# Transposing the first pair by blocks on VectorE and through DRAM, in a fused attention and Fourier kernel

## The chip, the cores and the metric

The kernel runs on one core of a Trainium2 chip. The metric is the device time of one execution in microseconds. Before the change it is 3119.44 us, the median of three runs (3116.04 to 3120.33).

## The reference, cut to what matters

The input x has 4 images of 64 channels, 96 by 96 positions, in float32. Two layers follow each other, each added to its input.

```
# layer 0, on the group-normalised x (N = 9216 positions)
q, k, v  = wq x + bq, wk x + bk, wv x + bv     # 8, 8 and 64 channels
out      = v . sigmoid(q^T k)                  # an N x N matrix for each image
out      = out + x;  scale = sigmoid(mlp(mean(out)) + mlp(max(out)))
x        = x + out * scale

# layer 1, on the group-normalised result
u_hat    = rfft2(u)                            # 96 x 49 modes
v_hat    = per mode (c -> o) matrix, for 32 rows (16 low, 16 high) x 16 columns of modes; the rest is 0
x        = x + irfft2(v_hat)
```

Nearly all the work is the N x N matrix of layer 0. Layer 1 keeps 32 x 16 modes, so its transforms are two small matrix products: along w to 16 modes (real and imaginary, 32 columns) and along h to 32 modes.

## The kernel before, in words

Two images are a pair, and a pair fills the 128 partitions (2 images x 64 channels). `xs[p]` is a 128 x 9216 tile that holds pair p, with positions h, w along the free dimension. The attention of the first pair runs first, then that of the second.

**Tiles and blocks.** A pair's attention has 18 blocks of 512 query positions (36 in all). A block has 144 chunks: 72 groups of 128 keys for each of two images. Chunks are handled in tiles of 6 or 7: TensorE writes 6 or 7 PSUM banks of energies (line 441), ScalarE takes their sigmoid into `at` (line 452), TensorE multiplies `at` with the values into an accumulating bank (line 470). PSUM has 8 banks, one of which accumulates. So a tile of 7 fills PSUM, and a tile of 6 leaves one bank spare. A block follows one of three patterns: DENSE (24 tiles of 6), HALF (22 tiles, about half of them of 6) or SPARSE (21 tiles, three of them of 6). `pattern` (line 530) gives each block its own: the second pair's first 12 blocks are HALF, its last six SPARSE. There are 774 tiles. Block 18, the second pair's first, begins with tile 384, in the code `first`.

**Hidden work.** During the second pair's attention, layer 1 of the first pair is woven in (class `Hidden`, line 236). Its steps are put at tile numbers when the program is written: `put` (line 545) takes a list of steps and gives each the next free slot at or after a tile, where a slot is a tile whose successor has size 6, so that a bank is spare. These steps stand in `mid[t]`, between the energies of tile t+1 and the products of tile t. Work that needs no bank goes to `end[t]`. The main loop (lines 646 to 663) emits a tile at a time in this order, and `later` ties a step's VectorE instructions behind the last marked VectorE instruction of the attention. One slot in a block goes to the queries of the next block.

The steps in their order, with the tiles that `put` gives them:
- `result(s)`, 12 strips of 768 positions, at the ends of tiles 391, 393, ..., 413: load the strip of the original x into `old`, combine (line 162), write the sum to DRAM (`x1d`), and take statistics.
- `transposes(r)`, 24 steps from tile 393 on: TensorE transposes four rows h of the image, 128 x 96 each, into a bank, and VectorE copies them to `xT` (96 x 512).
- `along_w(m)`, 6 steps among the former: four matmuls with the 96 x 32 table `fw` into four groups of 32 partitions of one bank. VectorE copies the bank to `ae`, and the DMA takes it through DRAM (`ad`) into `ah`, where h lies on the partitions. The last is at tile 475.
- statistics at tiles 477 to 483, then `along_h(i)` at tiles 493, 495, 497, 499: 32 matmuls each with weights 96 x 64 out of `ah` and 64 columns of the table `fh`, and two scalings by VectorE into `ut`.
- `mix` (16 steps from tile 503), `back_h` (8 steps from 551) and `back_w` (24 steps from 581 to 639) multiply by the modes' matrices, whose weights are loaded four at a time, and transform back.

All of these DMAs are issued by the SyncE queue (SP), in order: an issue that waits holds those behind it. When a step's bank, its VectorE copy or its operand isn't ready, TensorE waits too, since it takes its instructions in order. [...]

Of the kernel before, what the change touches and what calls it, by code (L numbers as in the profile page):

```python
# [33 lines left out]
F32 = mybir.dt.float32  # L34
F32R = mybir.dt.float32r
AF = mybir.ActivationFunctionType
ALU = mybir.AluOpType
# [3 lines left out]
P = 128  # L41
B, C, H, W = 4, 64, 96, 96
# [4 lines left out]
KW = 16  # L47
KH = 32
NB = 512
NBLK = N // NB  # L50
# [4 lines left out]
DENSE = [6] * 24  # L55
HALF = [6 if i == 1 or i % 2 == 0 and i < 18 else 7 for i in range(22)]
SPARSE = [6 if i in (0, 1, 11) else 7 for i in range(21)]
LAG = 8
SIDE = 4
U = KH * KW * 4  # L60
UPAD = 4 * SIDE
STRIP = 8 * W
SQ = 32
NSQ = H // SQ
NSTRIP = N // STRIP
# [16 lines left out]
def tile_kernel(ctx: ExitStack, tc: tile.TileContext, x, cst, late, spec, out):  # L82
    nc = tc.nc
    xf = x.rearrange("b c h w -> (b c) (h w)")
# [5 lines left out]
    dram = ctx.enter_context(tc.tile_pool(name="dram", bufs=1, space=bass.MemoryType.DRAM))  # L90
# [3 lines left out]
    xs = []  # L94
    for p in range(NPAIR):
        xt = xpool.tile([P, N], F32, tag=f"x{p}", name=f"x{p}")
        for s in range(9):
            cols = bass.ts(s, N // 9)
# [7 lines left out]
    def named(name, rows=P):  # L106
        return cs[:rows, PLACE[name]]

    pav, nhalf, low_sb, ident = named("pav"), named("nhalf"), named("low"), named("ident")
# [126 lines left out]
    class Hidden(Layer1):  # L236


        def __init__(self, p, gate, bank, move, work):
            super().__init__(p, gate, bank, move, (nc.sync,) * 3)  # L240
            self.work = work
            self.stats = small.tile([P, 2 * NSTRIP, 6], F32, tag="stats1", name=f"stats1_{p}")
            self.xts, self.ah = {}, None
            self.ad = dram.tile([H, 2 * KW, P], F32, tag=f"ad{p}", name=f"ad_{p}")
            self.zd = dram.tile([H, 2 * KW, 2, C], F32, tag=f"zd{p}", name=f"zd_{p}")

# [4 lines left out]
            self.wts = (self.wts + rooms[:3]) * (KH // 8)  # L251
            self.place_of_vt = lambda: rooms[3]

        def result(self, s):
            p, cols = self.p, bass.ts(s, STRIP)
            old = self.work.tile([P, STRIP], F32, tag="old", bufs=2, name=f"old_{p}_{s}")
            nc.sync.dma_start(old, xf[bass.ts(p, P), cols])
            self.combine(s, old)
            for i in (2 * s, 2 * s + 1):
                nc.vector.bn_stats(self.stats[:, i, :], xs[p][:, bass.ts(i, STRIP // 2)])  # L260

        def stats_steps(self):
            mr, steps, _ = group_stats(self.stats, self.bank, f"l1_{self.p}")
            return steps + [lambda: self.spread(mr)]

        def transposes(self, r):

            pt = self.bank(f"pt_{self.p}_{r}")
            for i in range(4):
                nc.tensor.transpose(pt[:W, bass.ts(i, P)], xs[self.p][:, bass.ts(4 * r + i, W)],  # L270
                                    ident)
            self.xts[r] = self.work.tile([W, NB], F32, tag="xT", bufs=4, name=f"xT_{self.p}_{r}")
            self.move(self.xts[r], pt[:W, :])

        def along_w(self, m):


            pa = self.bank(f"pa_{self.p}_{m}")
            for g in range(4):
                nc.tensor.matmul(pa[bass.ts(g, 2 * KW), :], named("fw", W), self.xts[4 * m + g],  # L280
                                 start=True, stop=True)
            ae = self.work.tile([P, NB], F32, tag="ae", bufs=2, name=f"ae_{self.p}_{m}")
            self.move(ae, pa)
            if self.ah is None:
                self.ah = self.work.tile([P, 2 * KW * P], F32, tag="ah", name=f"ah_{self.p}")
            for g in range(4):
                nc.sync.dma_start(
                    self.ad[16 * m + 4 * g:16 * m + 4 * g + 4].rearrange("i k c -> k i c"),
                    ae[bass.ts(g, 2 * KW), :].rearrange("k (i c) -> k i c", c=P))
            rows = bass.ts(m, 16)  # L290
            nc.sync.dma_start(self.ah[rows, :],
                                     self.ad[rows].rearrange("h k c -> h (k c)"))

        def along_h(self, i):

            b, half = i // 2, i % 2
            ah = self.ah.rearrange("h (s k b c) -> h s k b c", k=KW, b=2, c=C)
            u = self.ut[:, :U].rearrange("q (h k n s b) -> q n k s h b", h=KH, n=SIDE, s=2, b=2)
            if i == 0:
                nc.vector.memset(self.ut[:, U:], 0.0)  # L300
            pu = self.bank(f"pu_{self.p}_{i}")
            fh = named("fh", H)
            for k in range(KW // 2):
                for s in range(2):
                    for part in range(2):
                        first = KH * (2 - s - part)
                        nc.tensor.matmul(pu[bass.ts(part, C), bass.ts(k, 2 * KH)],
                                         ah[:H, s, half * (KW // 2) + k, b, :],
                                         fh[:, first:first + 2 * KH],
                                         start=(s == 0), stop=(s == 1))  # L310
            v = pu.rearrange("q (n k s h) -> q n k s h", n=2, s=2, h=KH)
            for n in range(2):
                nc.vector.tensor_scalar(u[:, 2 * half + n, :, :, :, b], v[:, n],
                                        self.rs[:, 0, b:b + 1], None, ALU.mult)

        def weights(self, rows):
            for h in rows:
# [38 lines left out]
    with tc.tile_pool(name="work", bufs=1) as work, \  # L356
# [32 lines left out]
        def later(step):  # L389
            with tc.issue_after(mark[0].ins):  # L390
                step()
# [126 lines left out]
        each, norm0, _ = stats_of(0)  # L518
# [5 lines left out]
        q = queries(0, 0)  # L524
# [2 lines left out]
        keys(0, 1)  # L527
        values_of(0, 1)

        pattern = [DENSE] + [SPARSE] * (NBLK - 2) + [DENSE] + [HALF] * 12  # L530
        pattern += [SPARSE] * (NPAIR * NBLK - len(pattern))
        sizes = [size for sz in pattern for size in sz]
        starts = [sum(sz[:i]) for sz in pattern for i in range(len(sz))]
# [7 lines left out]
        end = [[] for _ in range(T)]  # L541
# [3 lines left out]
        def put(t, steps, every=1):  # L545

            for step in steps:
                t = next(f for f in free if f >= t)
                free.remove(t)
                mid[t] += [lambda step=step: later(step)]  # L550
                t += every
            return t

        ask = {}
        for n in range(1, NPAIR * NBLK):
            t = begins[n] - 4
            if pattern[n - 1] is DENSE:
                end[t] += [lambda n=n: ask.update({n: queries(n // NBLK, n % NBLK)})]
            else:
                t = [f for f in free if f < begins[n] - 1][-1]  # L560
# [15 lines left out]
        for s in range(NBLK):  # L576
            tiles = TILES * (NBLK - 1) + 8 * (s + 1)
            t = next(t for t in range(T) if done[t] >= tiles)
# [5 lines left out]
        first = begins[NBLK]  # L584
        gate, steps, _ = after(0)
        end[first + 1] += [lambda: later(steps[0])]
        put(first + 2, steps[1:], 2)
        l1 = Hidden(0, gate, bank_a, lambda dst, src: nc.vector.tensor_copy(dst, src), work)  # L588
        x1d = dram.tile([P, N], F32, tag="x1", name="x1d")
        for s in range(NSTRIP):  # L590
            end[first + 7 + 2 * s] += [lambda s=s: later(lambda: (
                l1.result(s), nc.sync.dma_start(x1d[:, bass.ts(s, STRIP)],
                                                xs[0][:, bass.ts(s, STRIP)])))]
        t = put(first + 9, [step for m in range(H // 16) for step in [
            lambda r=r: l1.transposes(r) for r in range(4 * m, 4 * m + 4)] + [
                lambda m=m: l1.along_w(m)]])
        t = put(t, l1.stats_steps(), 2)

        def workspace():
# [10 lines left out]
            l1.weights(range(5, 8))  # L610

        end[t] += [workspace]
        t = put(t + 2, [lambda i=i: l1.along_h(i) for i in range(4)], 2)
        end[t] += [more_room, lambda: later(l1.constant_mode)]

        def mixing(q, half):
            l1.mix(q, half)
            if half and q + 2 < KH // 4:
                l1.weights(range(4 * q + 8, 4 * q + 12))

        t = put(t + 1, [lambda q=q, half=half: mixing(q, half)
                        for q in range(KH // 4) for half in range(2)])
        t = put(t + 5, [lambda i=i: l1.back_h(i // 4, i // 2 % 2, i % 2) for i in range(8)])
        t = put(t + 5, [lambda i=i: l1.back_w(i, x1d) for i in range(H // 4)])


        early = []
# [1 line left out]
        def fetch():  # L629
            held = xpool.tile([P, N], F32, tag="x0", name="w_early")  # L630
            early.extend(held[:, bass.ts(i, KW * C)] for i in range(9))
            for i, w in enumerate(early):
                nc.gpsimd.dma_start(w, spec[NSLOT + i])
# [4 lines left out]
        for s in range(NSTRIP):  # L638
            tiles = TILES * (NPAIR * NBLK - 1) + 2 * (STRIP // P) * (s + 1)
            t = next(t for t in range(T) if done[t] >= tiles)  # L640
# [5 lines left out]
        for t in range(T):  # L646
            n = block[t]
            spare[0] = n % 2 * 7
            if t + 1 < T:
                if starts[t + 1] == 0:  # L650
                    q = ask[n + 1]
# [5 lines left out]
            old = sum(1 for pair, _ in items if t and 2 * pair < total[t - 1])  # L657
# [6 lines left out]
        gate, steps, f = after(1)  # L664
# [4 lines left out]
    with tc.tile_pool(name="tail", bufs=1, reuse_waits="tile") as tail, \  # L669
# [19 lines left out]
        fw = lc[:, :NSQ * P]  # L689
        fh = lc[:, NSQ * P:3 * NSQ * P].rearrange("q (s m) -> q s m", s=2)  # L690
# [5 lines left out]
        def occupy(n, behind, pool):  # L696
# [3 lines left out]
            with tc.issue_after(behind.ins):  # L700
                for _ in range(n):
# [3 lines left out]
        l1 = Layer1(1, gate, lambda name: small_bank.tile([P, NB], F32, tag="m", name=name),  # L705
                    evacuate, (nc.sync, nc.gpsimd, nc.scalar))
# [10 lines left out]
        pu = [pu_bank.tile([P, NB], F32, tag=f"u{b}", name=f"pu_{b}") for b in range(2)]  # L717
        along_h = []
        for s in range(NSTRIP):
            cols = bass.ts(s, STRIP)  # L720
# [6 lines left out]
            n, i = divmod(s, NSTRIP // NSQ)  # L727
            if i == 0:
                pa = pa_bank.tile([P, 2 * NB], F32, tag="a", name=f"pa_{n}", bufs=2)
            v = xt.rearrange("q (h n c) -> q n h c", n=NSQ, c=SQ)  # L730
# [187 lines left out]
```

## Time and profile before

| part | from the profile |
|---|---|
| span of the profiled execution | 3116.6 us, 43034 instructions |
| TensorE (PE) busy | 3072.2 us, 99% |
| ScalarE (ACT) busy | 2424.6 us, 78% |
| VectorE (DVE) busy | 397.0 us, 13% |
| DMA, mean over the span | 29 GB/s, 88.87 MB |
| granted TensorE clock | 0.995 |
| second pair's blocks without hidden steps | 79.4 us each |
| second pair's blocks with hidden steps | 83.2 to 90.7 us each |
| from the last block's end to the end of the span | about 90 us |

The page names a group of instructions by its line, engine, operation and tiles (out<-in). PE is TensorE's matmuls and PEld its weight loads, which overlap them. A matmul of float32 data appears as two records. "Idle before" is the time for which an engine stood still before the instructions of a group, with the engine or DMA that ended it. A duration of one matmul overlaps its neighbours', so the cost of a step is read best from the distance between the energies (line 441) of two tiles that follow each other.

### The profile page before, as it was taken

The numbers are of one execution on the slowest core, as the hardware profiler recorded it, in microseconds if no ns is written. First come the engines' busy times: TensorE is split into PE (matmuls) and PEld (weight loads), VectorE is DVE, ScalarE is ACT, GpSimd is POOL, SyncE is SP. The second block draws the span as 40 slices with busy tenths as digits, with TensorE's granted clock in tenths as the row PEclk, the third lists the DMA queues.
The fourth block names the chain that finished last, engine by engine and source line by source line (L and its number), as shares of the span: only waits on it lengthen the run. The fifth ranks groups of instructions, "written<-read, shape, count | busy, mean of one in ns | idle before, by whom it ended". The sixth has DMA issues, their size and how long they took to land.

```text
span 3116.6 us, 43034 instructions
## 1 busy us (share of the span) xinstructions
PE 3072.2 (99%) x19186; PEld 1147.4 (37%) x19186; DVE 397.0 (13%) x838; ACT 2424.6 (78%) x1585; POOL 24.5 (1%) x49
## 2 busy tenths in 40 slices
PE   6999999999999999999999999999999999999998
PEld 3433333333333333334433333333333333333335
DVE  5300000000000000002331110110101100000015
ACT  3788888888888888886777777777777788888871
POOL 0000000000000000000000000000000010000001
PEclk9999999999999999999999999999999999999998
DMA  3000000000000000000120010131210130000026
GB/s 143 1 1 1 1 1 1 1 1 1 1 1 1 1 1 1 1 1 1 41 88 14 8 36 13 52 125 44 36 34 31 41 120 1 1 1 1 6 74 216
DMA packets 39161, 88.87 MB, mean 29 GB/s; under 512 B 10336, under 2 KB 17248, under 8 KB 38880
## 3 DMA queue, kind: packets, MB, share of 16 engines
q1 hardware_dynamic: 31856, 61.88, 6.4%
q0 software_dynamic: 5344, 19.27, 1.7%
q10 hardware_dynamic: 1776, 4.97, 0.4%
q8 instruction: 150, 2.46, 0.3%
q14 instruction: 35, 0.29, 0.0%
HBM read 62.77 MB, written 23.33 MB: 28 GB/s over the span
## 4 chain that ended last, share of the span: by engine, by line
PE 97%; DVE 1%; DMA 1%; issue 0%; POOL 0%; SPq 0%; ACT 0%; POOLq 0%; DVEq 0%
PE banks L470 74%; PE banks L441 16%; PE banks L409 1%; PE banks L421 1%; PE banks L348 1%; PE banks L398 1%; PE banks L203 1%; DMA x<-in_x_dram 0%; PE py L825 0%; PE banks L270 0%; DVE x L162 0%; DMA old<-in_x_dram 0%; DMA vd<-vm 0%; DVE xt L724 0%; PE banks L326 0%
## 5 line engine op out<-in xcount | busy, mean ns | idle before, releaser
L452 ACT ACTIVATE at<-banks 128x1536 f32<-128x1536 f32 (+1 forms) x1548 | 2404.4, 1597 | 610.6 <-PE banks L441 546.8
L470 PE MATMUL banks<-at,vT 128*64 128x512 f32 (+1 forms) x11728 | 2395.2, 549 | 0.0
L470 PEld LDWEIGHTS banks<-at,vT 128*64 128x64 f32 x11728 | 780.4, 136 | 1348.9 <-issue 1294.1
L441 PE MATMUL banks<-q,kT 32*128 32x512 f32 x5184 | 571.4, 454 | 1.6 <-DVE xT L588 1.6
L441 PEld LDWEIGHTS banks<-q,kT 32*128 32x128 f32 x5184 | 232.9, 182 | 472.3 <-issue 301.5
L475 DVE SCALAR_TENSOR_TENSOR x<-banks,x 128x512 f32<-128x512 f32 x36 | 24.9, 692 | 897.7 <-PE banks L470 897.7
L378 DVE TENSOR_SCALAR full_q<-banks,cs 128x256 f32<-128x256 f32 x36 | 17.4, 484 | 858.8 <-PE banks L421 858.8
L409 PE MATMUL banks<-cs,x 128*64 128x128 f32 x576 | 41.6, 287 | 1.5 <-DVE full_k L378 0.6
L431 DVE CAST q<-q 32x256 fp32r<-32x256 f32 x144 | 40.9, 284 | 3.9
L351 DVE TENSOR_TENSOR x<-banks,x 128x384 f32<-128x384 f32 x24 | 13.4, 558 | 197.0 <-PE banks L348 156.9
L409 PEld LDWEIGHTS banks<-cs,x 128*64 128x64 f32 x576 | 32.3, 141 | 16.2 <-DVE full_k L378 14.6
L588 DVE COPY xT<-banks 96x512 f32<-96x512 f32 x24 | 16.5, 686 | 167.1 <-PE banks L270 167.1
L386 DVE SCALAR_TENSOR_TENSOR q<-high_q,cs,full_q 64x256 fp32r<-64x256 f32 x72 | 34.6, 480 | 2.4
L378 DVE TENSOR_SCALAR full_k<-banks,cs 128x256 f32<-128x256 f32 x36 | 17.4, 484 | 93.2 <-PE banks L398 93.2
L588 DVE COPY ws<-banks 128x512 f32<-128x512 f32 x16 | 11.1, 692 | 141.7 <-PE banks L203 141.7
L412 DVE TENSOR_TENSOR vT<-banks,cs 128x512 f32<-128x512 f32 x36 | 24.8, 689 | 8.4 <-PE banks L409 8.3
L398 PE MATMUL banks<-x,cs 128*64 128x256 f32 x144 | 24.2, 396 | 1.6 <-DVE x L149 1.5
L477 DVE TENSOR_REDUCE maxs<-x 128x1 f32<-128x512 f32 x36 | 24.7, 686 | 1.2
L421 PE MATMUL banks<-x,cs 128*64 128x256 f32 x144 | 23.9, 410 | 0.6 <-DVE full_k L378 0.6
L483 DVE BATCH_NORM_STATS2 stats<-x 128x6 f32<-128x512 f32 x36 | 22.1, 679 | 8.0 <-DMA x<-in_x_dram 8.0
L732 PE MATMUL pa<-xt,lc 128*128 128x256 f32 x72 | 18.9, 422 | 3.6 <-DVE xt L724 2.6
L725 ACT ACTIVATE vT<-x,less 128x768 f32<-128x768 f32 x12 | 11.2, 934 | 12.4 <-DVE x L162 8.4
(117 smaller groups left out, 452.2 us busy)
## 6 DMA issues: line engine op xcount, KB each, us to landing
ws<-in_spec_dram SPq DMA_DIRECT2D x20, 512.0 KB
x<-in_x_dram SPq DMA_DIRECT2D x15, 512.0 KB
out_dram<-x SPq DMA_DIRECT2D x18, 384.0 KB
room<-in_spec_dram SPq DMA_DIRECT2D x12, 512.0 KB
w<-in_spec_dram POOLq DMA_DIRECT2D x10, 512.0 KB, 6.9
old<-in_x_dram SPq DMA_DIRECT2D x12, 384.0 KB
x1d<-x SPq DMA_DIRECT2D x12, 384.0 KB
x<-x1d SPq DMA_DIRECT2D x12, 384.0 KB
```

Of the source, the lines that this page charges most:

```text
L203: self.last = nc.tensor.matmul(pv[bass.ts(g, 32), :].rearrange("q (n k o) -> q n k o", n=SIDE, o=C)[:, :, k, :], self.ut[:, at:at + 32], s ...
L348: nc.tensor.matmul(py[bass.ts(b, C), :4 * W], self.z[:, i, bass.ts(b, C)], named("gw"), start=True, stop=True)
L378: nc.vector.tensor_scalar(u, src, bias, None, ALU.add)
L386: mark[0] = nc.vector.scalar_tensor_tensor(dst, h.bitcast(F32), is_low, u, ALU.mult, ALU.add)
L398: nc.tensor.matmul(pp[cols, :NB // 2], named("wk")[:, cols], src[:, e, :, :], start=True, stop=True)
L409: nc.tensor.matmul(pp[bass.ts(e, P // 2), bass.ts(i, P)], xs[p][:, bass.ts(2 * (4 * s + i) + e, P // 2)], named("wv"), start=True, stop=True)
L421: nc.tensor.matmul(pq[rows, :half], named("wq")[:, rows], xs[p][:, n * NB + e * half:n * NB + (e + 1) * half], start=True, stop=True)
L431: nc.vector.tensor_copy(q[to:to + 32, cols], q[of:of + 32, cols])
L441: nc.tensor.matmul(banks[:, bank_of(t) + i - starts[t], :], kT[r:r + 32, i // 4, :], q[r:r + 32, :], start=True, stop=True)
L452: nc.scalar.activation(at[:, of + lo:of + hi, :], banks[:, bank + lo:bank + hi, :], AF.Sigmoid)
L470: nc.tensor.matmul(acc[half, cols], vT[:, j, half], at[:, place(2 * pair + b), cols], start=(j == 0), stop=(j == NCH - 1))
L588: l1 = Hidden(0, gate, bank_a, lambda dst, src: nc.vector.tensor_copy(dst, src), work)
```

## The change

The first pair's layer 1 gets its transposes in another way, and its transform along h is written anew:
- `fetch(s)` loads strip s one strip ahead of its `result`.
- `result(s, x1d)` combines as before and writes `x1d`; VectorE then transposes the strip in 32 x 32 blocks into the buffer `old`, and the DMA writes it to a DRAM tile `xd`. `turned(s)` reads it back with three DMAs that put the blocks where a full transpose would have them: `xT` is now 96 x 1024 for a strip, two buffers. The runs that are contiguous on both sides have 32 floats. `transposes` is gone.
- `along_w` reads the strips instead of rows; it is otherwise the same.
- `along_h(b)` has two steps, one for each image of the pair, instead of four. The table `fh` is now the stationary operand (96 x 32) and `ah` the moving one (512 columns): 8 matmuls a step into four groups of 32 partitions. VectorE transposes the bank in blocks and scales it into `ut` with three instructions.
- The schedule: results come at tiles 391 + 6s, `turned` at 393 + 6s, `along_w(m)` at the first free slot from 406 + 12m on (407, 419, 431, 449, 455, 471). One HALF block becomes SPARSE, which makes 773 tiles in all. The last step, `back_w(23)`, has tile 625 where it had 639.

It is meant to take the transposes and part of the transform along h off TensorE, and to need fewer tiles with a spare bank.

```diff
+        def fetch(self, s):
+            p = self.p
+            self.olds[s] = self.work.tile([P, STRIP], F32, tag="old", bufs=2, name=f"old_{p}_{s}")
+            nc.sync.dma_start(self.olds[s], xf[bass.ts(p, P), bass.ts(s, STRIP)])
+
+        def result(self, s, x1d):
+            cols, old = bass.ts(s, STRIP), self.olds[s]
+            if s + 1 < NSTRIP:
+                self.fetch(s + 1)
             self.combine(s, old)
+            nc.sync.dma_start(x1d[:, cols], xs[self.p][:, cols])
+            nc.vector.transpose(old, xs[self.p][:, cols])
+            nc.sync.dma_start(self.xd[s], old)
...
+        def turned(self, s):
+            self.xts[s] = self.work.tile([W, STRIP // W * P], F32, tag="xT", bufs=2,
+                                         name=f"xT_{self.p}_{s}")
+            for n in range(NSQ):
+                nc.sync.dma_start(
+                    self.xts[s][bass.ts(n, SQ), :].rearrange("w (h k c) -> w h k c", k=4, c=SQ),
+                    self.xd[s].rearrange("(k w) (h n c) -> n w h k c", k=4, n=NSQ, c=SQ)[n])
...
-        def transposes(self, r):
-            pt = self.bank(f"pt_{self.p}_{r}")
-            for i in range(4):
-                nc.tensor.transpose(pt[:W, bass.ts(i, P)], xs[self.p][:, bass.ts(4 * r + i, W)],
-                                    ident)
-            self.xts[r] = self.work.tile([W, NB], F32, tag="xT", bufs=4, name=f"xT_{self.p}_{r}")
-            self.move(self.xts[r], pt[:W, :])
...
-                nc.tensor.matmul(pa[bass.ts(g, 2 * KW), :], named("fw", W), self.xts[4 * m + g],
+                nc.tensor.matmul(pa[bass.ts(g, 2 * KW), :], named("fw", W),
+                                 self.xts[2 * m + g // 2][:, bass.ts(g % 2, NB)],
                                  start=True, stop=True)
...
+            for s in range(2):
+                for part in range(2):
+                    first = KH * (2 - s - part)
+                    for k in range(2):
+                        nc.tensor.matmul(pu[bass.ts(2 * part + k, SQ), :], fh[:, first:first + KH],
+                                         ah[:H, s, :, b, bass.ts(k, SQ)],
                                          start=(s == 0), stop=(s == 1))
+            t = self.work.tile([P, NB], F32, tag="ae", bufs=2, name=f"t_{self.p}_{b}")
+            nc.vector.transpose(t, pu)
...
-        pattern = [DENSE] + [SPARSE] * (NBLK - 2) + [DENSE] + [HALF] * 12
+        pattern = [DENSE] + [SPARSE] * (NBLK - 2) + [DENSE] + [HALF] * 11
...
+        end[first + 3] += [lambda: l1.fetch(0)]
         for s in range(NSTRIP):
+            end[first + 7 + 6 * s] += [lambda s=s: later(lambda: l1.result(s, x1d))]
+            end[first + 9 + 6 * s] += [lambda s=s: l1.turned(s)]
+        for m in range(H // 16):
+            t = put(first + 22 + 12 * m, [lambda m=m: l1.along_w(m)])
...
-        t = put(t + 2, [lambda i=i: l1.along_h(i) for i in range(4)], 2)
+        t = put(t + 2, [lambda b=b: l1.along_h(b) for b in range(2)], 2)
...
-        t = put(t + 5, [lambda i=i: l1.back_w(i, x1d) for i in range(H // 4)])
+        t = put(t + 8, [lambda i=i: l1.back_w(i, x1d) for i in range(H // 4)])
```

More of the change, by code (lines that the diff above doesn't have):

```diff
@@ L242, in __init__ @@
             self.stats = small.tile([P, 2 * NSTRIP, 6], F32, tag="stats1", name=f"stats1_{p}")
-            self.xts, self.ah = {}, None
+            self.olds, self.xts, self.ah = {}, {}, None
+            self.xd = dram.tile([NSTRIP, P, STRIP], F32, tag=f"xd{p}", name=f"xd_{p}")
             self.ad = dram.tile([H, 2 * KW, P], F32, tag=f"ad{p}", name=f"ad_{p}")
@@ L252, in more_room @@
             self.place_of_vt = lambda: rooms[3]
[L254 to L257, printed above, removed]
+        def fetch(self, s):
[6 more added lines that the diff above has]
+                self.fetch(s + 1)
             self.combine(s, old)
+            nc.sync.dma_start(x1d[:, cols], xs[self.p][:, cols])
+            nc.vector.transpose(old, xs[self.p][:, cols])
+            nc.sync.dma_start(self.xd[s], old)
             for i in (2 * s, 2 * s + 1):
-                nc.vector.bn_stats(self.stats[:, i, :], xs[p][:, bass.ts(i, STRIP // 2)])
+                nc.vector.bn_stats(self.stats[:, i, :], xs[self.p][:, bass.ts(i, STRIP // 2)])
+        def turned(self, s):
[5 more added lines that the diff above has]
+                    self.xd[s].rearrange("(k w) (h n c) -> n w h k c", k=4, n=NSQ, c=SQ)[n])
         def stats_steps(self):
@@ L292, in along_w, with along_h @@
                                      self.ad[rows].rearrange("h k c -> h (k c)"))
-        def along_h(self, i):
-            b, half = i // 2, i % 2
+        def along_h(self, b):
             ah = self.ah.rearrange("h (s k b c) -> h s k b c", k=KW, b=2, c=C)
-            u = self.ut[:, :U].rearrange("q (h k n s b) -> q n k s h b", h=KH, n=SIDE, s=2, b=2)
-            if i == 0:
+            u = self.ut[:, :U].rearrange("q (h k n s b) -> q n k h s b", h=KH, n=SIDE, s=2, b=2)
+            if b == 0:
@@ L300, in along_h @@
                 nc.vector.memset(self.ut[:, U:], 0.0)
-            pu = self.bank(f"pu_{self.p}_{i}")
+            pu = self.bank(f"pu_{self.p}_{b}")
             fh = named("fh", H)
[L303 to L309, printed above, removed]
-                                         start=(s == 0), stop=(s == 1))
@@ L311, in along_h @@
[L311 to L314, printed above, removed]
+            for s in range(2):
[4 more added lines that the diff above has]
+                                         ah[:H, s, :, b, bass.ts(k, SQ)],
+                                         start=(s == 0), stop=(s == 1))
@@ new lines, in along_h @@
+            t = self.work.tile([P, NB], F32, tag="ae", bufs=2, name=f"t_{self.p}_{b}")
+            nc.vector.transpose(t, pu)
+            t = t.rearrange("q (n k h) -> q n k h", n=SIDE, h=KH)
+            lo, hi = slice(0, C), slice(C, P)
+            nc.vector.tensor_scalar(u[:, :, :, :, 0, b], t, self.rs[:, 0, b:b + 1], None, ALU.mult)
+            nc.vector.tensor_scalar(u[lo, :, :, :, 1, b], t[hi], self.rs[hi, 1, b:b + 1], None,
+                                    ALU.mult)
+            nc.vector.tensor_scalar(u[hi, :, :, :, 1, b], t[lo], self.rs[lo, 0, b:b + 1], None,
+                                    ALU.mult)
@@ L589, in tile_kernel @@
         x1d = dram.tile([P, N], F32, tag="x1", name="x1d")
+        end[first + 3] += [lambda: l1.fetch(0)]
         for s in range(NSTRIP):
[L591 to L596, printed above, removed]
+            end[first + 7 + 6 * s] += [lambda s=s: later(lambda: l1.result(s, x1d))]
+            end[first + 9 + 6 * s] += [lambda s=s: l1.turned(s)]
+        for m in range(H // 16):
+            t = put(first + 22 + 12 * m, [lambda m=m: l1.along_w(m)])
         t = put(t, l1.stats_steps(), 2)
```

## The prediction, made before the result was known

> **What bounds the kernel now.** I read the busy table first, then the chain of waits, the groups by line, and last the timeline of TensorE around single steps of the hidden work.
>
> ```profile
> PE 3072.2 (99%) x19186; PEld 1147.4 (37%) x19186; DVE 397.0 (13%) x838; ACT 2424.6 (78%) x1585; POOL 24.5 (1%) x49
> PE 97%; DVE 1%; DMA 1%; issue 0%; POOL 0%; SPq 0%; ACT 0%; POOLq 0%; DVEq 0%
> ```
> TensorE is busy 99% of the span and is 97% of the chain that ended last. So a microsecond of matmul that goes is a microsecond of span, and a wait of TensorE costs as much as it lasts. VectorE (13%) and the DMA queues cost nothing until TensorE waits for them. Next the groups that the change touches (columns: instructions, busy us, mean ns, idle before):
>
> ```profile
> L270 PE MATMUL banks<-cs,x 128*96 128x128 f32 x96 | 15.4, 282 | 0.0
> L588 DVE COPY xT<-banks 96x512 f32<-96x512 f32 x24 | 16.5, 686 | 167.1 <-PE banks L270 167.1
> L280 PE MATMUL banks<-xT,cs 96*32 96x512 f32 x48 | 6.4, 605 | 0.0
> L307 PE MATMUL banks<-cs,ah 96*64 96x64 f32 x256 | 8.3, 224 | 0.0
> ```
> The transposes (L270) are on TensorE and so on the path; their copies (L588) are not. Busy time of a group overlaps its neighbours, so I price a step by how far it moves the next tile's energies (L441):
>
> ```profile
> 1706.29 0.73 PE L441 MATMUL banks<-q,kT 32*128 32x512 f32 x6
> 1706.95 1.06 PE L280 MATMUL banks<-xT,cs 96*32 96x512 f32 x8
> 1707.94 2.79 PE L470 MATMUL banks<-at,vT 128*64 128x512 f32 x12
> 1710.67 0.73 PE L441 MATMUL banks<-q,kT 32*128 32x512 f32 x7
> ...
> 1714.49 0.73 PE L441 MATMUL banks<-q,kT 32*128 32x512 f32 x6
> 1715.15 0.64 PE L270 MATMUL banks<-cs,x 128*96 128x128 f32 x4
> 1715.72 2.80 PE L470 MATMUL banks<-at,vT 128*64 128x256 f32 x16
> 1718.45 0.73 PE L441 MATMUL banks<-q,kT 32*128 32x512 f32 x7
> ```
> ```profile
> 2164.05 0.73 PE L441 MATMUL banks<-q,kT 32*128 32x512 f32 x6
> 2164.71 2.80 PE L470 MATMUL banks<-at,vT 128*64 128x256 f32 x16
> 2167.45 0.73 PE L441 MATMUL banks<-q,kT 32*128 32x512 f32 x7
> ```
> An unused free slot takes 3.39 us (2164.05 to 2167.45, and the same at the other unused slots). With four transposes it takes 3.96 us, with one transform along w 4.38 us. Steps therefore add in full: 0.574 us for a group of four transposes (median of the 24, against 3.388), 0.997 for along_w. There is no gap of TensorE in which they hide. The four along_h tiles last 5.25 to 5.26 us: 1.867 each.
>
> One place shows TensorE waiting for VectorE, which waited for a strip:
>
> ```profile
> 1615.85 1.02 DVE L162 SCALAR_TENSOR_TENSOR x<-x,gate,old 128x768 f32<-128x768 f32 x1 [4.98 <-DMA old<-in_x_dram]
> 1616.78 0.68 DVE L588 COPY xT<-banks 96x512 f32<-96x512 f32 x1
> 1617.52 0.49 PE L441 MATMUL banks<-q,kT 32*128 32x512 f32 x1 [1.59 <-DVE xT L588]
> ```
> The copy of tr4 stood behind a combine that had no strip yet; that tile took 5.91 us instead of 3.82: 2.09 us lost, once.
>
> [...] the second pair's block transposes of 128x768 (L724) take 958 ns, and the change needs the DMA to put the blocks in place. [...] The trace has no 128 B run. Its 256 B writes (zd) took 18 ns a packet, 512 B writes (ad) 33, and the 512 B strided reads out of DRAM (z from zd) 82 ns, 768 of them in 6.7 us.
>
> **The change, part by part.**
> *Transposes off TensorE.* 24 x 0.574 = 13.8 us of path removed. In their place 12 VectorE transposes at 0.958 (L724's row) = 11.5 us, and 24 copies of 0.686 = 16.5 us go. VectorE is idle some 87% of the span, so both count as nothing.
>
> *along_h.* Before, 4 x 1.867 = 7.5 us. After, two steps of 8 matmuls of 96x32 weights by 512 columns, spread over four column groups, twice round. One round is what along_w does (four matmuls, 96x32 by 512, four column groups): 0.997. So 2 x 2 x 0.997 = 4.0 us, and 3.5 us saved. The strided moving operand (16 runs of 32 floats) I price at nothing: the second pair's L732 reads runs alike at 422 ns for 256 columns. The evacuation becomes a transpose out of PSUM (0.69, as L813) and three scalings of about 0.65 (L778, L780), 2.6 us a step on VectorE; the bank is free after the first, two tiles before the next step wants it.
>
> *Prefetch.* The strip for result(s+1) is asked for six tiles (23 us) early, and results come every six tiles instead of two. The wait above goes: 2.1 us. It would only stay if the queue were blocked; see below.
>
> *One HALF pattern less.* Block 28 (2375.2 to 2460.5 us between its first energies and the next block's) takes 85.35 us with eight back_w steps of 0.645, so 80.19 bare; a SPARSE block takes 79.39. Saved: 0.8 us. Counting slots through put(), the last back_w then comes at tile 625, at the start of the first SPARSE block, so nothing is pushed out.
>
> Sum: 13.8 + 3.5 + 2.1 + 0.8 = **20.2 us**, if no new wait arises.
>
> *The new wait.* along_w(m) needs strips 2m and 2m+1 back from DRAM. Each strip is 128x768 floats in runs of 32: 3072 runs of 128 B, 192 for each of 16 DMA engines. Bounds: [...] 192 x 18 = 3.5 (256 B writes), 192 x 82 = 15.7 us (the DRAM reads a packet), and 27 us if the 768 reads in 6.7 us are a rate of the queue. I take some 35 ns, near the 512 B writes: about 7 us, since the 82 ns belong to reads with a 64 KB pitch and on few partitions. Slots from put(): along_w at tiles 407, 419, 431, 449, 455, 471; strips are asked for at 393 + 6s. xT has two buffers, so the load of strip 2m also waits for along_w(m-1) and holds the SP queue in the meantime. Mostly that leaves 8 tiles, 31 us, for the later strip. The tight one is along_w(4): a query step takes slot 443, so along_w(3) comes at 449, strips 8 and 9 both start there, and along_w(4) asks for them at 455, some 22 us later. Two loads at T each, about 3 us of issue and landing (up to 9 if strip 9's trip to DRAM queues behind strip 8): no wait up to T = 9.5 us (6.5 in the worse order). At 7 us it is hidden or costs 1 us. Queued behind on SP are the prefetch of strip 10, ad writes and ah loads; none is wanted before tile 451, and along_h comes 12 tiles after the last along_w. Weights for mixing are asked for 12 tiles before use.
>
> **Rivals.**
> *A: along_w(4) waits.* T of 10 to 15.7 us gives a TensorE wait of 2 x T + 3 - 22 = 1 to 12 us (18 in the worse order): 3100 to 3117, middle 3106. For it: the only DRAM reads of small runs in the trace are the slow ones. Against: their pitch.
> *B: slower.* At 27 us a strip the DMA needs 12 x 27 = 324 us, and from tile 393 to 471 there are 78 x 3.85 = 300; with two buffers that wait on each other every along_w is late, 12 tiles (46 us) against 54 for two strips plus latency: 6 x 8 = 48 us lost less some slack, say 30 to 40, against 20 gained: 3110 to 3135, middle 3127. For it: the rate of 6.7 us for 768 reads was measured. Against: those reads go to 8 partitions, the new ones to 32 at a time.
> *C: only the transposes count.* The new along_h runs no better than the old (rows of 32 weights instead of 64), or a wait of VectorE stays: 13.8 + 0.8 = 14.6 us, 3104.8.
>
> **How the numbers follow.** Forecast 72%: 3119.4 - 20.2 = 3099.2. A 16%, B 5%, C 7%. Medians of three scatter by about 2 us either way (3116.0 to 3120.3 before), so the forecast alone spans 3096 to 3102; the range takes in C and the lower half of A: 3095.5 to 3108. Slower by over 0.2% (past 3125.7) needs most of B: 4%. Within 0.2% (above 3113.2): the top of A and the low end of B, 4%. Faster: 92%.
>
> **What would show it.** No L270 group; TensorE's along_w tiles still near 4.38 us, and the one at tile 455 too if no wait arises; along_h as two tiles of about 5.4 us; 773 tiles; no tile of 5.9 us near 1615 us; VectorE's combine with no wait for old; packets of 128 B, 36,864 of them, with their own duration, which settles T. The prediction is wrong if an along_w waits for xT, if the load of a strip lasts over 10 us, or if a tile without a step takes longer than 3.39 or 3.82 us.

## The result, and the profile after

| | before | changed |
|---|---|---|
| median | 3119.38 us (3116.04 to 3120.33, 4 runs) | 3096.68 us (3096.3 to 3096.89, 4 runs) |
| profiled span | 3116.6 us | 3095.1 us |
| second pair, first energies of block 18 to those of block 35 | 1431.50 us | 1410.92 us |

The ratio of the runs is 0.9929, with a 95% interval of 0.9912 to 0.9946; the medians differ by 22.7 us. Forecast were 3099.2 us and a range of 3095.5 to 3108.

The busy table and the chain of the changed kernel answer to the first lines shown of the kernel before:

```profile
PE 3052.5 (99%) x18866; PEld 1131.9 (37%) x18866; DVE 391.5 (13%) x826; ACT 2421.6 (78%) x1583; POOL 24.5 (1%) x49
PE 98%; DVE 1%; DMA 1%; issue 0%; ACT 0%; POOL 0%; SPq 0%; ACTq 0%; DVEq 0%
```

TensorE is still busy 99% and is still the path; its busy time fell by 19.7 us (3072.2 to 3052.5). VectorE, which took over the transposes, has 5.5 us less to do than before. The lines moved by 17 with the change (L441 is now L458, L470 is L487). The groups by line of the changed kernel:

```profile
L268 DVE STREAM_TRANSPOSE old<-x 128x768 f32<-128x768 f32 x12 | 11.6, 968 | 0.1
L291 PE MATMUL banks<-xT,cs 96*32 96x512 f32 x48 | 6.4, 605 | 0.0
L320 PE MATMUL banks<-ah,cs 96*32 96x512 f32 x32 | 3.8, 598 | 0.0
L324 DVE STREAM_TRANSPOSE t<-banks 128x512 f32<-128x512 f32 x2 | 1.4, 716 | 22.0 <-PE banks L320 15.8 <-ACT at L469 6.3
```

The transposes' group (L270) is gone from TensorE. The 12 block transposes (L268) last 968 ns each, with 0.1 us of waiting in all. The new along_h (L320) is busy 3.8 us where the old was 8.3. Now its tile in TensorE's timeline, and an along_w tile, along_w(4), with the issues (SPq) of its two strips:

```profile
1883.88 0.73 PE L458 MATMUL banks<-q,kT 32*128 32x512 f32 x6
1884.55 1.92 PE L320 MATMUL banks<-ah,cs 96*32 96x512 f32 x16
1886.40 2.80 PE L487 MATMUL banks<-at,vT 128*64 128x256 f32 x16
1889.13 0.73 PE L458 MATMUL banks<-q,kT 32*128 32x512 f32 x7
```
```profile
1758.78 5.19 SPq L278 DMA_DIRECT2D xT<-xd  x6
...
1779.22 0.73 PE L458 MATMUL banks<-q,kT 32*128 32x512 f32 x6
...
1779.88 1.07 PE L291 MATMUL banks<-xT,cs 96*32 96x512 f32 x8
```

From 1883.88 to 1889.13 the along_h tile takes 5.25 us; there are two of them (5.246 and 5.240) instead of four. The second fence is the tight place of the prediction, along_w(4): strips 8 and 9 are asked for at 1758.78 and their last packet is done at 1766.2, while along_w(4) starts at 1779.88. So 13.6 us of slack stood where the prediction had expected next to none. All six along_w tiles last 4.383 to 4.386 us, the 5.91 us tile is gone, and no tile without a step is longer than 3.83 us. What a strip's trip back costs stands in the packet records: 36,864 packets of 128 B of 13 ns in the median, and 2.7 to 3.1 us from the first packet to the last for a strip that is alone. Three strips took longer (3.5, 5.3 and 5.1 us), with loads of `old` or `ah` in flight beside them.

### The profile page after: what moved, and what is told of

Read it like the earlier page. It is cut to its first block, busy times and chain, and to the rows that moved or that the text cites. A ratio compares the mean times of both kernels' runs of the same rounds, so it can differ in the third digit from the quotient of the medians.

```text
span 3095.1 us, 42450 instructions
## 1 busy us (share of the span) xinstructions
PE 3052.5 (99%) x18866; PEld 1131.9 (37%) x18866; DVE 391.5 (13%) x826; ACT 2421.6 (78%) x1583; POOL 24.5 (1%) x49
## 4 chain that ended last, share of the span: by engine, by line
PE 98%; DVE 1%; DMA 1%; issue 0%; ACT 0%; POOL 0%; SPq 0%; ACTq 0%; DVEq 0%
PE banks L487 75%; PE banks L458 17%; PE banks L426 1%; PE banks L438 1%; PE banks L365 1%; PE banks L415 1%; PE banks L203 1%; DMA x<-in_x_dram 0%; PE py L841 0%; PE pv L203 0%; DVE x L162 0%; DVE xt L740 0%; PE banks L343 0%; PE banks L291 0%; PE pz L822 0%
## 5 line engine op out<-in xcount | busy, mean ns | idle before, releaser
L487 PE MATMUL banks<-at,vT 128*64 128x512 f32 (+1 forms) x11728 | 2394.8, 549 | 0.0
L487 PEld LDWEIGHTS banks<-at,vT 128*64 128x64 f32 x11728 | 780.5, 136 | 1356.4 <-issue 1301.6
L458 PE MATMUL banks<-q,kT 32*128 32x512 f32 x5184 | 569.9, 453 | 0.0
L458 PEld LDWEIGHTS banks<-q,kT 32*128 32x128 f32 x5184 | 232.1, 183 | 468.6 <-issue 314.0
```

The costliest lines, as they stand in the source:

```text
L458: nc.tensor.matmul(banks[:, bank_of(t) + i - starts[t], :], kT[r:r + 32, i // 4, :], q[r:r + 32, :], start=True, stop=True)
L487: nc.tensor.matmul(acc[half, cols], vT[:, j, half], at[:, place(2 * pair + b), cols], start=(j == 0), stop=(j == NCH - 1))
```

## The experiments

The times of one kernel spread by 0.6 to 8.4 us from lowest to highest, but the second pair's stretch, from the first energies of block 18 to those of block 35, repeats to 0.1 us (1410.92 and 1410.88 in the two profiles of the changed kernel; each other kernel has one profile). I compare single terms by it; for each profile it is read from the start of the energies (line 441 of the kernel before).

**The old transform along h in the changed kernel.**
```diff
-        pattern = ... + [HALF] * 11
+        pattern = ... + [HALF] * 12
-        t = put(t + 2, [lambda b=b: l1.along_h(b) for b in range(2)], 2)
+        t = put(t + 2, [lambda i=i: l1.along_h(i) for i in range(4)], 2)   # along_h of the kernel before
```
Expected: 

> The changed kernel with the old transform along h (four steps of 32 matmuls) and twelve HALF blocks, which its longer list of steps needs. If steps add in full to the path, as the prediction has it, four tiles of 5.25 us stand in place of two of 5.24, 3.76 us more, and the twelfth HALF block costs 0.8: 4.6 us over the changed kernel, about 3101.3 us. The rival, that the long matmuls gained nothing and the transposes gave it all, expects 3097.5 us (the HALF block alone).


Measured: 3102.13 us (3102.03 to 3103.03), ratio to before 0.9945 (0.9933 to 0.9958); stretch 1415.47 us, 4.55 more than the changed kernel. The steps add in full; the long matmuls earn their own share.

**Twelve HALF blocks in the changed kernel.** The first line of the diff above alone.
Expected: 

> The changed kernel with twelve HALF blocks again. The prediction's term: 80.19 us against 79.39 for that block, 0.8 us slower than the changed kernel, 3097.5 us. The rival, that a tile more or less costs nothing by itself, expects the block at 79.4 us.


Measured: 3098.64 us (3096.59 to 3099.31), ratio 0.9932 (0.9918 to 0.9946); stretch 1411.69 us, and block 29 takes 80.83 us with one back_w in it where it took 80.04: 0.77 to 0.79 us. So along_h alone is 1415.47 - 1411.69 = 3.78 us.

**The kernel before with strips asked for one ahead.**
```diff
-            nc.sync.dma_start(old, xf[bass.ts(p, P), cols])        # in result(s)
+            if s + 1 < NSTRIP:
+                self.fetch(s + 1)
...
+        end[first + 3] += [lambda: l1.fetch(0)]
```
Expected: 

> The kernel before, and nothing changed but that each strip is asked for one result ahead. The prediction's reason, that the late strip was cured by asking for it earlier, expects the 5.91 us tile near 1615 us to become 3.82: 2.1 us faster than before, no combine that waits for a strip. The rival: with two buffers the strips were asked for as soon as a buffer was free anyway, and the strip came late because four results follow each other in one cluster and a load then shares the DMA engines with the transfers of ah; then the wait stays, in the same size, and only spreading the results takes it away.


Measured: 3116.61 us (3115.63 to 3117.37, 13 runs) against 3118.6, ratio 0.9993 (0.9985 to 1.0001), which the times alone don't tell from no change; stretch 1429.41 us, 2.09 less, all of it the tile that took 5.91 us and now takes 3.82. Its timeline at that place:

```profile
1611.43 1.02 DVE L162 SCALAR_TENSOR_TENSOR x<-x,gate,old 128x768 f32<-128x768 f32 x1 [1.62 <-DMA old<-in_x_dram]
1611.68 0.64 PE L276 MATMUL banks<-cs,x 128*96 128x128 f32 x4
...
1612.96 0.67 DVE L594 COPY xT<-banks 96x512 f32<-96x512 f32 x1
...
1614.98 0.74 PE L447 MATMUL banks<-q,kT 32*128 32x512 f32 x7
```
The combine still waits for its strip (1.62 us, not 4.98), but it is through before the transposes' copy is due, and the energies (L447) find their bank free. The prediction's reason holds here.

**The changed kernel with each strip asked for in its own result.**
```diff
-            if s + 1 < NSTRIP:
-                self.fetch(s + 1)
+            self.fetch(s)
...
-        end[first + 3] += [lambda: l1.fetch(0)]
```
Expected: 

> The changed kernel with each strip asked for in its own result. If asking ahead is what keeps the combine from waiting, VectorE waits for strips again and TensorE loses up to 2 us in one or more tiles: 3098 to 3100 us. The rival, that the wider spacing of the results does it, expects no tile longer than in the changed kernel: 3096.7 us.


Measured: 3096.38 us (3095.33 to 3099.53), ratio 0.9927 (0.9915 to 0.994); stretch 1410.88 us, no longer tile, and no combine that waits for a strip. So asking ahead does nothing in the changed kernel: either cure is enough alone, and the wider spacing was there anyway.

**TensorE's transposes with the rest of the change.** The kernel before with strips asked for ahead and the new along_h.
Expected: 

> The kernel before with the strips asked for ahead and the new transform along h, but TensorE's transposes and twelve HALF blocks: all of the change but the transposes and the block. By adding terms: 3119.4 - 2.1 - 3.8 = 3113.5 us. The distance to the changed kernel with twelve HALF blocks is then the transposes alone, 13.8 us. If moving the transposes cost something of its own on VectorE or the DMA, the distance is smaller.


Measured: 3119.03 us (3114.37 to 3119.72, 13 runs), ratio 0.9999 (0.999 to 1.0007); stretch 1430.85 us where 1425.6 was expected. The first back_w had moved, and in the order of TensorE's instructions it and the next queries stood among the energies of a tile:

```profile
2260.97 0.81 PE L359 MATMUL banks<-cs,ws 128*64 128x384 f32 x4
2262.75 0.51 PE L452 MATMUL banks<-q,kT 32*128 32x512 f32 x4 [0.96 <-ACT at L463]
2265.26 0.51 PE L452 MATMUL banks<-q,kT 32*128 32x512 f32 x3 [2.00 <-ACT at L463]
2265.69 0.65 PE L432 MATMUL banks<-x,cs 128*64 128x256 f32 x4
2266.17 4.01 PE L481 MATMUL banks<-at,vT 128*64 128x512 f32 x12
```
The energies (L452) stand in pieces and wait for the sigmoids (0.96 and 2.00 us), and then the products take 4.01 us where they take 2.8 elsewhere. The tiles are 5.19 and 8.46 us long. That run says nothing on the transposes; with the last line of the change's diff it does:

```diff
-        t = put(t + 5, [lambda i=i: l1.back_w(i, x1d) for i in range(H // 4)])
+        t = put(t + 8, [lambda i=i: l1.back_w(i, x1d) for i in range(H // 4)])
```
Expected: 

> The kernel before with the strips asked for ahead, the new transform along h, and back_w three tiles later (the last line of the diff), still with TensorE's transposes and twelve HALF blocks. In the run without that line the first back_w stood six tiles after the last back_h, TensorE's written order there had its matmuls between the energies of a tile, and two tiles lost 5.8 us. If that is why the gain was missing, those two tiles go back to 4.03 and 3.82 us, the second pair's stretch is 1431.5 - 2.1 - 3.8 = 1425.6 us and the time 3113.4 us; the 13.9 us from there to the changed kernel with twelve HALF blocks (1411.7) are then the transposes. If the long tiles come again elsewhere, the cause is another.


Measured: 3111.33 us (3106.55 to 3114.97, 7 runs) against 3118.19, ratio 0.9972 (0.9961 to 0.9983); stretch 1425.47 us, no long tile. From here to the changed kernel with twelve HALF blocks are 1425.47 - 1411.69 = 13.78 us: the transposes.

**How slow may the trip through DRAM be?** Three kernels read each strip back in shorter runs, with as many more DMAs; the order of the data is the same.
```diff
             for n in range(NSQ):
+                for j in range(R):                      # R = 2, 4, 8
+                    run = bass.ts(j, SQ // R)
                     nc.sync.dma_start(... "w (h k c) -> w h k c" ...[:, :, :, run],
                                       ... "(k w) (h n c) -> n w h k c" ...[n][:, :, :, run])
```
Expected, 16 floats: 

> The changed kernel, each strip read back in runs of 16 floats (64 B) by six DMAs instead of 32 floats by three: 6144 runs a strip. At the 13 ns a packet that 128 B runs took, T is about 5 us plus issue. The prediction's threshold for a wait of along_w(4) is T = 9.5 us, so no wait: 3096.7 us.


Expected, 8 floats: 

> The same in runs of 8 floats (32 B) by twelve DMAs a strip: 12288 runs. At 13 ns a packet T is 10 us; at 0.7 us an issue, twelve issues take 8.4 us, so T is 9 to 11 us, at the threshold: along_w(4) waits for 0 to 3 us, 3096.7 to 3100 us. If packets have no floor and cost by bytes, T stays at the issue time and nothing waits.


Expected, 4 floats: 

> The same in runs of 4 floats (16 B) by 24 DMAs a strip: 24576 runs, 1536 on each engine. At 13 ns a packet T is 20 us, 24 issues take 17 us. By the prediction's arithmetic along_w(4) waits 2 x 20 + 3 - 22 = 21 us, the other along_w not (12 tiles are 46 us for two strips): about 3118 us, all of it at one tile. The rival, that there is much more slack than counted, since results and loads run ahead of the tiles they are written at, expects a wait of under 10 us.

| run | packet, median | a strip (first to last packet) | median time, ratio to before | stretch |
|---|---|---|---|---|
| 128 B (the change) | 13 ns | 2.7 to 5.3 us | 3096.68, 0.9929 | 1410.92 us |
| 64 B | 11 ns | 4.8 to 7.1 us | 3097.33, 0.9934 (0.9919 to 0.995) | 1411.22 us |
| 32 B | 9 ns | 9.2 to 11.6 us | 3098.19, 0.9935 (0.9922 to 0.9949) | 1412.53 us |
| 16 B | 9 ns | 19.3 to 21.7 us | 3135.67, 1.0055 (1.0041 to 1.0068) | 1449.16 us |

At 64 and 32 B no along_w waits for its strips, though at 32 B it is close: strip 9's last packet is done at 1780.6, and along_w(4) starts at 1782.09. What they lose is 0.03 to 0.06 and 0.24 to 0.30 us in each along_w. With 32 B, the weight loads of along_w take 0.46 us from the first to the last, where they took 0.16 in the changed kernel; what sets them apart is not shown. The matmuls into the four column groups overlap less with it: they take 1.36 us where the changed kernel's took 1.07 (L295 is along_w, in the kernel with runs of 8 floats):

```profile
1602.22 1.36 PE L295 MATMUL banks<-xT,cs 96*32 96x512 f32 x8
```
At 16 B it falls apart. The tile of along_w(4), at TensorE, with the windows before, in and after the wait (the last three columns are granted clock, DMA share and GB/s):

```profile
1796.05 1.05 PE L295 MATMUL banks<-xT,cs 96*32 96x512 f32 x4
1815.17 1.92 PE L295 MATMUL banks<-xT,cs 96*32 96x512 f32 x4 [18.07 <-DMA ad<-ae]
1817.02 3.74 PE L491 MATMUL banks<-at,vT 128*64 128x512 f32 x12
```
```profile
1780.00:1796.00 16.00, 16.00 (x98) 5.58 (x94) 6.18 (x11) 13.01 (x10) 0.00 (x0) 1.00 0.73 21
1797.00:1815.00 18.00, 0.10 (x2) 0.00 (x0) 0.00 (x0) 0.45 (x1) 0.00 (x0) 0.54 0.73 27
1815.20:1818.00 2.80, 2.80 (x8) 0.52 (x10) 0.69 (x1) 0.00 (x0) 0.00 (x0) 0.50 0.86 304
```
The releaser that the trace names is the landing just before (ad from ae); packets of 16 B ran until 1814.6, and the matmuls went on at 1815.17, so it is strip 9 that along_w waited for. This tile lost 20.9 us (25.30 against 4.39), where 21 were expected; that the two agree is in part luck: the wait itself is 18.1 us, and the rest is the step in two halves and the lower clock after it. T was near 20 us as expected, though not for the packets, which took 9 ns and not 13: the 24 issues of a strip held the SP queue for 19.5 to 20.6 us.

Two more along_w lost time where nothing was expected. along_w(1) waited 3.02 us for a strip, and its tile lost 7.1 us: both of its strips start only after the along_w before, and strip 3 only 4.5 us after the end of strip 2, so 2 x 20 + 5 us meet some 44. At along_w(2), which lost 6.6 us, and 2.8 in the tile after it, the strips came in time (the last packet at 1696.6), and it was a load of the original x that came late:

```profile
1696.99 1.33 PE L295 MATMUL banks<-xT,cs 96*32 96x512 f32 x8
1698.21 1.02 DVE L162 SCALAR_TENSOR_TENSOR x<-x,gate,old 128x768 f32<-128x768 f32 x1 [9.27 <-DMA old<-in_x_dram]
1703.70 1.02 DVE L162 SCALAR_TENSOR_TENSOR x<-x,gate,old 128x768 f32<-128x768 f32 x1 [2.56 <-DMA old<-in_x_dram]
1706.55 0.67 DVE L609 COPY ae<-banks 128x512 f32<-128x512 f32 x1
1707.28 1.22 PE L462 MATMUL banks<-q,kT 32*128 32x512 f32 x7 [6.23 <-DVE ae L609]
```
The load of `old` was issued at 1694.07, behind strip 5's issues, which had held the SP queue since 1674.31. Two combines waited for their strips, the copy of along_w's bank (L609) stood behind them on VectorE, and the energies (L462) waited 6.23 us for that bank. It is the wait of the kernel before again, and the blocked queue that the prediction had named as what could bring it back. So the threshold holds for the tight pair (no wait with 9.3 us a strip, a long one with 19.4); the others were not as safe as the prediction had them.

**A version that goes further.**
```diff
-            end[first + 7 + 6 * s] ... end[first + 9 + 6 * s]
+            end[first + 7 + 4 * s] ... end[first + 9 + 4 * s]
-            t = put(first + 22 + 12 * m, [lambda m=m: l1.along_w(m)])
+            t = put(first + 18 + 8 * m, [lambda m=m: l1.along_w(m)])
-        pattern = ... + [HALF] * 11
+        pattern = ... + [HALF] * 10
```
Expected: 

> A version that goes further: results every four tiles instead of six, along_w every eight instead of twelve, and since the hidden work then ends 22 tiles earlier, ten HALF blocks instead of eleven. If T is near 3 us, no along_w waits, and the block that turns SPARSE saves 0.8 us: 3095.9 us. If the closer spacing makes an along_w or a combine wait, 3097 us or more.


Measured: 3105.78 us (3102.96 to 3107.81), ratio 0.9957 (0.9945 to 0.997); stretch 1418.06 us, 8 more than hoped. Not a transfer but the order of TensorE's instructions is the loss; around along_w(1):

```profile
1618.16 0.73 PE L458 MATMUL banks<-q,kT 32*128 32x512 f32 x6
1618.82 1.05 PE L291 MATMUL banks<-xT,cs 96*32 96x512 f32 x4
1619.80 2.79 PE L487 MATMUL banks<-at,vT 128*64 128x512 f32 x12
1622.53 0.73 PE L458 MATMUL banks<-q,kT 32*128 32x512 f32 x6
1623.19 1.05 PE L291 MATMUL banks<-xT,cs 96*32 96x512 f32 x4
```
Both strips had landed by 1608.4, yet along_w stands in two halves, a tile apart, and no wait stands before the second half. The source writes the four matmuls together; what set them apart is not shown. Half an along_w takes 0.98 us of path like a whole one (two column groups of four), and its bank stays taken a tile longer, so the energies wait for the copy (at 1625.17 the weight load of one had waited 0.81 us for it). Four of the six were split in this way. With the first along_w two tiles of free slots later (409 instead of 405) all six stand whole:

```diff
-            t = put(first + 18 + 8 * m, [lambda m=m: l1.along_w(m)])
+            t = put(first + 24 + 8 * m, [lambda m=m: l1.along_w(m)])
```
Expected: 

> The closer spacing again (results every four tiles, along_w every eight, ten HALF blocks), but the first along_w two tiles later, which leaves the four matmuls of each along_w next to each other in TensorE's written order; in the first attempt four of the six stood in two halves with a tile's products between them. If the halves were the loss, all six tiles are near 4.38 us and the kernel stands 0.8 us under the changed one: 3095.9 us, a second pair's stretch of 1410.2 us against 1410.9. The rival, that the closer spacing itself makes VectorE or the DMA late, expects some of the 8 us again.


Expected of the changed kernel beside it: 

> The changed kernel as it is, as the reference for the two others on the same chip: 3096.7 us, and 20.6 us less than the kernel before in the stretch between the first energies of the second pair and those of its last block.


Measured: 3095.56 us (3093.83 to 3098.18), ratio 0.9929 (0.9916 to 0.9941), stretch 1410.12 us; the changed kernel 3096.77 us (3096.4 to 3097.25), ratio 0.9931 (0.9919 to 0.9944), stretch 1410.88 us. By the stretch the closer version is 0.76 us ahead, as forecast; the times alone don't resolve that.

## Why the prediction was right

Each term of its sum was isolated (predicted, measured by the stretch):

| term | predicted | measured | from |
|---|---|---|---|
| transposes off TensorE | 13.8 us | 13.78 | all but the transposes, less twelve HALF blocks |
| along_h | 3.5 us | 3.78 | old along_h, less twelve HALF blocks |
| the late strip | 2.1 us | 2.09 | asked for ahead, from before |
| one HALF block less | 0.8 us | 0.77 | twelve HALF blocks, from the change |
| sum | 20.2 us | 20.42 | whole stretch: 20.58 |

- *Bound and additivity.* Steps in free slots cost what they cost alone. That VectorE's work and the copies count as nothing held: removing and adding them left the other tiles at 3.39 and 3.82 us.
- *along_h* was priced at two rounds of along_w, 1.99 us a step; it took 1.855 (5.243 less 3.388). The small error of the sum is there, and rival C, in which the new along_h gains nothing, is out. The strided moving operand cost nothing, as assumed (598 ns a matmul, L320, against 605 for along_w's, L291). VectorE's transpose out of PSUM took 0.72 and its scalings 0.66 to 0.68 us.
- *Prefetch.* The size was right, and prefetch does cure the wait in the kernel before. But in the change the spacing cures it too; the prediction named both and could not tell that one alone would do.
- *The trip through DRAM.* T was taken as 7 us and is 2.7 to 3.1 for a strip alone, 5.3 at most. That term was off by a factor of two, and it cost nothing, since even 9.3 us (strips 8 and 9 with 32 B runs) were hidden. The packet takes 13 ns in the median, and none of the 36,864 took under 11, where the prediction chose 35 ns. The 82 ns of the reads of zd say nothing on these reads; which of pitch and partitions slows those was not tried. The order of the two strips at along_w(4) was the better one. Rivals A and B were wrong for this change. With T near 20 us A came about, and so did B's slower kernel (ratio 1.0055), but not B's way there: two of the six along_w waited for their strips, not all. The prediction had seen that prefetches stand behind the strips in the same queue, but asked only at the tight pair whether one is wanted; with 16 B runs that cost 9.4 us at along_w(2).
- *Profile against time.* The profiled spans differ by 21.5 us and the medians by 22.7. Of the 0.9 us outside the stretch nothing was changed by the diff; the time before and after it varies by more between the two profiles of the changed kernel (1511.20 and 1512.68 us before it, 172.94 and 171.62 after). So the sum is confirmed by the stretch; the medians' 22.7 us, 2.5 more than forecast, are not resolved that finely.

## What to carry to other kernels

Where one engine is busy all the time, price every edit by the distance that it moves that engine's next recurring instruction, not by busy time or mean duration: four such differences added up to the change of the stretch within half a microsecond. Work may then be moved off that engine to idle ones, here even by a round trip through DRAM in 128 B runs, as long as its latency (7.5 us from the first issue to the last packet of two strips, against 21 us until they are used) fits between the slots, and as long as it doesn't hold up other loads of the same queue. Check the order of the bound engine's instructions after any change of slots: twice here a step in pieces cost 5.4 and 7.9 us without any transfer being late.

## What was not expected of the hardware

- *Runs under 128 B.* The median packet takes 13, 11, 9 and 9 ns for 128, 64, 32 and 16 B: from 32 B down it gets no shorter. There the SP queue's issues fill the time. At 9 ns the 768 and 1536 packets of each DMA engine would make 6.9 and 13.8 us a strip, an estimate, and strips took at least 9.2 and 19.3. Each DMA of 1024 runs holds the queue 0.56 to 0.69 us when nothing backs up; with 32 B runs the 24 for both strips of along_w(4) took 18.0 us, and with 16 B runs the 24 for one strip took 19.5 to 20.6.
- *A wait of TensorE can cost more than it lasts*, where the prediction had it at as much. With 16 B runs along_w(1) waited 3.02 us and its tile lost 7.1. Of the other 4.1 some 1.0 is the step in two halves (0.98 in the closer version), and the rest goes with the clock: from 1648.9 to 1655.5 the granted clock was 0.53, the second half of the step took 1.92 us instead of 1.05, and the products took 4.98 us instead of 2.80. From 1656 to 1660 it was 1.00 again. The windows above show a lower clock with the long wait (0.54 in it, 0.50 after it), and so does the long tile of the run with a misplaced back_w (0.56 after waits of 0.96 and 2.00 us with 0.5 us of matmuls between them). After the 1.59 us wait in the kernel before it stayed at 1.00. How long a wait must be for the clock to fall was not measured.
